# Patch embedding by three products for two neighbouring patches, with its tokens on the partitions, and one set of statistics for two layernorms in a row

## The chip, the core and the metric

The kernel runs on one core of a Trainium2 chip. The metric is the time of one execution on the device in microseconds (us), as the median of three runs. All data are fp32.

The core's engines have queues of their own and run each queue in order. TensorE (PE in the profile, its weight loads PEld) multiplies matrices, VectorE (DVE) and ScalarE (ACT) do elementwise work and reductions, GpSimd (POOL) does small or slow elementwise work, and SyncE (SP) issues transfers. A matmul keeps a stationary operand of 128x128 in the array and streams a moving operand of up to 512 columns through it; its result goes to PSUM. Each fp32 matmul of the program stands in the profile as two instructions, each transpose as one.

## The reference, cut to what matters

```python
# tokenizer: patches of 16 steps, 8 apart, of x [4, 64, 512, 64] (batch, channel, time, variable)
xp = pad(x, 8 more steps at the end, mode="edge")
patches = xp[:, :, idx, :]                        # idx = n * 8 + 0..15, n = 0..63
xf = rfft(patches over the 16 steps, norm="ortho")   # 9 frequencies
h = concat([xf.real, xf.imag]) @ W.T              # [4, 64 variables x 64 patches, 256]

# layer 0: attention with a decaying memory, then an MLP
a = layernorm(h)                                  # first of two in a row, no gain
y = layernorm(a) * g1 + b1
q, k, v = y @ Wq.T + bq, y @ Wk.T + bk, y @ Wv.T + bv
mem[t] = decay * mem[t - 1] + k[t] * v[t]         # over the 4096 tokens of a batch
a = a + q * mem
a = a + relu((layernorm(a) * g2 + b2) @ W1.T + b1) @ W2.T + b2
h = h + a

# experts: the best two of eight, weights by softmax
t = layernorm(h)
h = h + t + sum over e of combine[:, e] * (gelu(t @ w1[e]) @ w2[e])
```

A layernorm subtracts the mean over 256 features and divides by sqrt(variance + 1e-5).

## The kernel before

The DFT is linear, so it is folded into the embedding's weights at the start: `weff[(h c), m, d]`, with `m = 0..7` for the steps of a patch in two halves of four (L90 to L95, 128 VectorE instructions). A token is then the sum over eight `m` of products with 128 rows (two sub-steps times 64 channels) of x.

Each batch has 4096 tokens, cut into 8 blocks of 512 (`BLK`, four tiles of 128, `TT = 4`); there are 32 blocks in all. The tokens run over variables first and patches second. One batch of x lies in SBUF as `xt` (a single buffer, L64); `load_x` for the next batch waits until the last block of this one has read it.

The work of a block is in two generators, whose `yield`s cut it into steps. `attention` (L165) has nine steps: 0 the embedding, features on the partitions (L174, two times eight matmuls with 512 columns, copied with a permutation at L181); 1 eight transposes to tokens (L190, L191) and two layernorms in a row (`z`, `zz`); 2 transposes of `zz` to features (`to_features`, L150); 3 k, v, the scan and q (L162, L212); 4 eight transposes back (L230), the residual, a layernorm, and GpSimd's additions to h (L235, L236); 5 transposes; 6 the MLP's first product (L162 with `w_sb`, activations into the buffer `aT`, L244); 7 its second product (L250), the sum (L257) and a layernorm; 8 transposes of those tokens to `tokT` and the routing (`route`, matmuls L273, 17 small VectorE instructions, `comb`).

`experts` (L305) has nine steps too: the hidden layer of expert 0 (`hidden`, L162 with `ew_sb` and the gelu at L313); then the transposes of `comb` (L321, copied to `combT`, L323), the biases (L328), and for each expert the second product (L337), the weighted sum into h (L346) and the hidden layer of the expert after next. The output goes out in one transfer per block (L354).

What runs beside what is set by the last loop: the experts of a block run step by step between the steps of the next block's attention, experts first in each step. Each engine's queue follows roughly from this order.

```python
for _ in zip_longest(before, attention(state, xt, blk, carry)):
    pass
before = experts(b=b, blk=blk, **state)
```

A layernorm is `bn_stats` and `bn_aggr` for each of four tiles on VectorE (L136, L137), the reciprocal root by `pow` on GpSimd (L139, L140), and four normalisations on VectorE (L142). PSUM has four buffers named `mm`, three named `tm` and one named `sm`. The pool `one` has one buffer for each name.

## Time and profile before

| | |
|---|---|
| median of three runs | 4033.25 us (4033.03 to 4033.52) |
| span of the profiled execution | 4034.0 us |
| mean granted TensorE clock | 0.982 of full speed |
| TensorE busy | 3835.9 us, 95% |
| VectorE busy | 1315.3 us, 33% |
| ScalarE busy | 882.2 us, 22% |
| GpSimd busy | 413.4 us, 10% |
| read from and written to HBM | 43.49 MB, 16.78 MB |

A row of the groups of instructions reads: line, engine, operation, tiles written and read, shapes, count, then busy time in us and mean ns of one, then the engine's idle time ahead of them and what ended it. A row in order of time reads: start in us, duration in us, engine, line, operation, tiles, and in brackets the idle time ahead of it and what ended it. Consecutive equal instructions are merged, and a matmul's duration overlaps with the next one's. A row of the busy time of stretches reads: the stretch, its length, busy us and instructions of PE, PEld, DVE, ACT and POOL, the granted TensorE clock, the DMA share and GB/s.

### The profile page before, as it was taken

What the parts mean: (1) busy time and instruction counts of PE and PEld (TensorE: products, weight loads), DVE (VectorE), ACT (ScalarE), POOL (GpSimd) and SP (SyncE); (2) the same over time, 40 slices, a digit from 0 to 9 for tenths busy, and PEclk for the clock granted to TensorE, in tenths of its full rate; (3) what the DMA queues carried; (4) which work ended last, traced back from release to release, by engine and by line L of the source; (5) the groups of instructions that cost most, each with busy time, mean ns of one, the idle gap of its engine ahead of it and who ended that gap; (6) DMA issues with size and microseconds to landing.
All of it is one profiled execution on the core that took longest, in us unless ns stands there. A gap on an engine that the chain in (4) does not pass through costs nothing. (4 is left out here: it accounts for less than half of the span.)

```text
span 4034.0 us, 32892 instructions
## 1 busy us (share of the span) xinstructions
PE 3835.9 (95%) x13184; PEld 2380.1 (59%) x13184; DVE 1315.3 (33%) x3712; ACT 882.2 (22%) x1248; POOL 413.4 (10%) x559
## 2 busy tenths in 40 slices
PE   2899999999999999999999999999999999999999
PEld 1466566665566565666665665656566656666566
DVE  5223332233333233322333322333233333223232
ACT  0122212222222222122222222222222221222222
POOL 0111110110101110101101011101011010011010
PEclk9899999999999999999999999999999999999999
DMA  6000000004000000001200000000400000000000
GB/s 178 0 6 1 6 6 6 6 6 85 6 6 6 6 1 6 6 6 38 58 1 6 6 6 6 6 1 6 90 6 6 1 6 6 6 6 6 1 6 11
DMA packets 61561, 62.37 MB, mean 15 GB/s; under 512 B 3800, under 2 KB 61152, under 8 KB 61408
## 3 DMA queue, kind: packets, MB, share of 16 engines
q1 hardware_dynamic: 52352, 50.86, 5.3%
q10 hardware_dynamic: 9056, 9.41, 0.9%
q8 instruction: 103, 1.69, 0.2%
q14 instruction: 50, 0.41, 0.0%
HBM read 43.49 MB, written 16.78 MB: 15 GB/s over the span
## 5 line engine op out<-in xcount | busy, mean ns | idle before, releaser
L337 PE MATMUL tm<-ew_sb,ge 128*128 128x256 f32 x4096 | 957.3, 388 | 0.0
L162 PE MATMUL mm<-tokT,ew_sb 128*128 128x512 f32 x2048 | 934.6, 597 | 0.0
L337 PEld LDWEIGHTS tm<-ew_sb,ge 128*128 128x128 f32 x4096 | 789.1, 196 | 145.4 <-issue 43.1
L346 DVE SCALAR_TENSOR_TENSOR h<-tm,comb,h 128x256 f32<-128x256 f32 x1024 | 451.4, 475 | 943.0 <-PE tm L337 942.0
L313 ACT ACTIVATE ge<-mm,vec 128x512 f32<-128x512 f32 x512 | 348.4, 687 | 1334.8 <-PE mm L162 1334.4
L162 PEld LDWEIGHTS mm<-tokT,ew_sb 128*128 128x128 f32 x2048 | 382.8, 191 | 363.8 <-issue 353.1
L174 PE MATMUL mm<-xt,weff 128*128 128x512 f32 x1024 | 447.7, 595 | 63.4 <-DMA xt<-in_x 63.4
L162 PE MATMUL mm<-hT,w_sb 128*128 128x512 f32 x1024 | 447.6, 595 | 0.7 <-ACT hT L154 0.7
L250 PE MATMUL tm<-w_sb,aT 128*128 128x256 f32 x2048 | 447.2, 379 | 0.0
L250 PEld LDWEIGHTS tm<-w_sb,aT 128*128 128x128 f32 x2048 | 389.1, 190 | 53.3 <-issue 0.5
L174 PEld LDWEIGHTS mm<-xt,weff 128*128 128x128 f32 x1024 | 195.7, 191 | 310.0 <-issue 245.0
L162 PEld LDWEIGHTS mm<-hT,w_sb 128*128 128x128 f32 x1024 | 195.6, 191 | 247.3 <-issue 238.2
L162 PE MATMUL mm<-hT,wqkv_sb 128*128 128x512 f32 x768 | 336.6, 594 | 0.2 <-ACT hT L154 0.2
L139 POOL TENSOR_SCALAR rstd<-mv 128x4 f32<-128x4 f32 x128 | 29.2, 228 | 2583.4 <-DVE mv L137 2583.4
L150 PE MATMUL mm<-ident,zz 128*128 128x128 f32 x768 | 178.6, 342 | 119.0 <-DVE zz L142 119.0
L162 PEld LDWEIGHTS mm<-hT,wqkv_sb 128*128 128x128 f32 x768 | 146.5, 191 | 184.8 <-issue 176.3
L150 PEld LDWEIGHTS mm<-ident,zz 128*128 128x128 f32 x768 | 107.8, 163 | 226.2 <-DVE zz L142 166.6
L244 ACT ACTIVATE aT<-mm,vec 128x512 f32<-128x512 f32 x256 | 175.9, 687 | 266.8 <-PE mm L162 266.8
L152 ACT COPY tokT<-mm 128x512 f32<-128x512 f32 x64 | 34.4, 589 | 686.7 <-PE mm L150 686.7
L235 POOL TENSOR_TENSOR h<-h,z 128x256 f32<-128x256 f32 x128 | 90.2, 726 | 914.8 <-ACT ge L313 867.9
L257 DVE TENSOR_TENSOR h<-tm,h 128x512 f32<-128x512 f32 x64 | 44.3, 692 | 379.2 <-PE tm L250 379.2
L181 ACT COPY ret<-mm 128x512 f32<-128x512 f32 x64 | 66.8, 1043 | 401.9 <-PE mm L174 401.9
(61 smaller groups left out, 1858.9 us busy)
## 6 DMA issues: line engine op xcount, KB each, us to landing
xt<-in_x SPq DMA_DIRECT2D x32, 1024.0 KB, 18.5
out<-h SPq DMA_DIRECT2D x32, 512.0 KB, 2.9
ew_sb<-in_ew ACTq DMA_DIRECT2D x2, 2048.0 KB, 31.1
w_sb<-in_w ACTq DMA_DIRECT2D x2, 1024.0 KB, 20.4
wf<-in_wtok ACTq DMA_DIRECT2D x2, 576.0 KB, 12.4
wf<-in_wtok ACTq DMA_DIRECT2D x2, 448.0 KB, 14.2
wqkv_sb<-in_wqkv ACTq DMA_DIRECT2D x1, 768.0 KB, 16.6
xt<-in_x SPq DMA_DIRECT2D x8, 64.0 KB, 14.3
```

The costliest lines, as they stand in the source:

```text
L150: nc.tensor.transpose(ps[:, ts(t, P)], src[:, t, ts(k, P)], ident)
L152: nc.scalar.copy(dst[:, k, :], ps)
L162: nc.tensor.matmul(ps, lhsT=w[:, k, ts(m, P)], rhs=rhs[:, k, :], start=k == 0, stop=k == KD - 1)
L174: nc.tensor.matmul(ps, lhsT=weff[:, m, ts(k, P)], rhs=xt[:, n0 : n0 + N, j * V + v0 : j * V + v0 + nv], start=m == 0, stop=m == 7,)
L181: nc.scalar.copy(hF[:, k, :].rearrange("p (v n) -> p n v", n=N), ps.rearrange("p (n v) -> p n v", n=N))
L235: nc.gpsimd.tensor_tensor(h[:, t, :], h[:, t, :], z[:, t, :], ALU.add)
L244: nc.scalar.activation(aT[:, m, :], ps, AF.Relu, bias=vec[:, MB1 + m : MB1 + m + 1])
L250: nc.tensor.matmul(ps[:, i, :], lhsT=aT[:, k, ts(t2 * 2 + i, P)], rhs=w2_sb[:, k, :], start=k == 0, stop=k == KH - 1,)
L257: nc.vector.tensor_tensor(h[:, ts(t2, 2), :], ps, h[:, ts(t2, 2), :], ALU.add)
L313: nc.scalar.activation(ge[:, m, :], ps, AF.Gelu, bias=vec[:, c : c + 1])
L337: nc.tensor.matmul(ps[:, i, :], lhsT=ge[:, k, ts(t2 * 2 + i, P)], rhs=ew2_sb[:, e, k, :], start=k == 0, stop=k == KD - 1,)
L346: nc.vector.scalar_tensor_tensor(h[:, t, :], ps[:, i, :], comb[:, t, e : e + 1], h[:, t, :], ALU.mult, ALU.add)
```

## The change

Two neighbouring patches, even and odd, share half of their steps: the second half of the even one is the first half of the odd one. With x0, x1, x2 for three consecutive groups of eight steps and W0, W1 for the two halves of the weights, the two tokens are x0 W0 + x1 W1 and x1 W0 + x2 W1. The change computes (x0 - x1) W0, (x2 - x1) W1 and, for both, x1 (W0 + W1).

- `wsum` (W0 + W1) is made once at the start.
- A new first step of `attention` makes the two differences on VectorE and a copy of x1 on ScalarE, for four sub-steps each, into a tile in the buffer named `aT`, in the order of the tokens.
- The embedding's matmuls have these as the stationary operand and the weights as the moving one, so that tokens come out on the partitions. The transposes at L190 and the permuted copies at L181 go. Each sum of two products is added to the common one on VectorE.
- The tiles of tokens are now even and odd patches apart; `hT` is written and `ret` read with a stride of 2, so that the scan has the tokens in order, and the output has two transfers per block.
- The first two layernorms use one set of statistics: the second one's variance is v / (v + eps), so both reciprocal roots come from v.
- `attention` has ten steps now and `experts` still nine.
- The scan writes into `ks`; the tile `mem` goes.

The diff, without the comments that it drops:

```diff
+        wsum = const.tile([P, J, D], F32)
+        nc.vector.tensor_tensor(wsum, weff[:, 0:J, :], weff[:, J:, :], ALU.add)
...
+    def layernorms(once, twice, src):
+        st = small.tile([P, TT, 6], F32, name="st")
+        mv = small.tile([P, TT, 2], F32, name="mv")
+        for t in range(TT):
+            nc.vector.bn_stats(st[:, t, :], src[:, t, :])
+            nc.vector.bn_aggr(mv[:, t, :], st[:, t, :])
+        rstd2 = small.tile([P, 2, TT], F32, name="rstd2")
+        nc.gpsimd.tensor_scalar(rstd2[:, 0, :], mv[:, :, 1], EPS, None, ALU.add)
+        nc.gpsimd.tensor_scalar(rstd2[:, 1, :], mv[:, :, 1], 1.0 + EPS, EPS * EPS, ALU.mult, ALU.add)
+        nc.gpsimd.tensor_tensor(rstd2, rstd2, mhalf2, ALU.pow)
+        for i, dst in ((1, twice), (0, once)):
+            for t in range(TT):
+                nc.vector.tensor_scalar(
+                    dst[:, t, :], src[:, t, :], mv[:, t, 0:1], rstd2[:, i, t : t + 1], ALU.subtract, ALU.mult
+                )
...
     def attention(state, xt, blk, carry):
         v0, nv = blk * BLK // N, BLK // N
-        hF = one.tile([P, KD, BLK], F32, name="ret")
-        for k in range(KD):
-            ps = p_mm.tile([P, BLK], F32, name="mm")
-            for m in range(8):
-                n0, j = m // J, m % J
-                nc.tensor.matmul(ps, lhsT=weff[:, m, ts(k, P)],
-                    rhs=xt[:, n0 : n0 + N, j * V + v0 : j * V + v0 + nv], start=m == 0, stop=m == 7)
-            nc.scalar.copy(
-                hF[:, k, :].rearrange("p (v n) -> p n v", n=N), ps.rearrange("p (n v) -> p n v", n=N)
-            )
+        xs = one.tile([P, 3, J, BLK // 2], F32, name="aT")
+        for j in range(J):
+            seg = xt[:, :, j * V + v0 : j * V + v0 + nv]
+            even, odd, after = seg[:, 0:N:2, :], seg[:, 1:N:2, :], seg[:, 2 : N + 1 : 2, :]
+            dst = [xs[:, i, j, :].rearrange("p (v n) -> p n v", n=N // 2) for i in range(3)]
+            nc.vector.tensor_tensor(dst[0], even, odd, ALU.subtract)     # L202
+            nc.vector.tensor_tensor(dst[1], after, odd, ALU.subtract)    # L203
+            nc.scalar.copy(dst[2], odd)                                  # L204
         yield
         h = two.tile([P, TT, D], F32, name="h")
-        for t2 in range(TT // 2):
+        ps = p_tm.tile([P, 2, D], F32, name="tm")
+        for u in range(TT // 2):
+            for j in range(J):
+                nc.tensor.matmul(
+                    ps[:, u, :], lhsT=xs[:, 2, j, ts(u, P)], rhs=wsum[:, j, :], start=j == 0, stop=j == J - 1
+                )
+        ms = one.tile([P, 2, D], F32, name="ms")
+        nc.scalar.copy(ms, ps)
+        for u in range(TT // 2):
             ps = p_tm.tile([P, 2, D], F32, name="tm")
             for i in range(2):
-                for k in range(KD):
-                    nc.tensor.transpose(ps[:, i, ts(k, P)], hF[:, k, ts(t2 * 2 + i, P)], ident)
-            nc.scalar.copy(h[:, ts(t2, 2), :], ps)
+                for j in range(J):
+                    nc.tensor.matmul(ps[:, i, :], lhsT=xs[:, i, j, ts(u, P)],
+                        rhs=weff[:, i * J + j, :], start=j == 0, stop=j == J - 1)
+            nc.vector.tensor_tensor(
+                h[:, ts(u, 2), :], ps, ms[:, u : u + 1, :].to_broadcast([P, 2, D]), ALU.add
+            )
+        yield
         z = one.tile([P, TT, D], F32, name="z")
-        layernorm(z, h)
         zz = two.tile([P, TT, D], F32, name="zz")
-        layernorm(zz, z)
+        layernorms(z, zz, h)
         yield
         hT = one.tile([P, KD, BLK], F32, name="hT")
-        to_features(hT, zz, G1, B1)
+        to_features(hT, zz, G1, B1, scan=True)     # written with a stride of 2
...
-                    nc.tensor.transpose(ps[:, i, ts(k, P)], ret[:, k, ts(t2 * 2 + i, P)], ident)
+                    nc.tensor.transpose(ps[:, i, ts(k, P)], ret[:, k, t2 * 2 * P + i : (t2 + 1) * 2 * P : 2], ident)
...
-        nc.sync.dma_start(out=out[b, ts(blk, BLK), :].rearrange("(t p) d -> p t d", p=P), in_=h)
+        to = out[b, ts(blk, BLK), :].rearrange("(u q r) d -> u q r d", q=P, r=2)
+        for u in range(TT // 2):
+            nc.sync.dma_start(out=to[u], in_=h[:, ts(u, 2), :])
```

In the changed kernel the transposes of `to_features` stand at L172, the feature products at L188, the routing matmuls at L309, the transposes of `comb` at L357, the biases at L364, the experts' second product at L373 and the MLP's second product at L286.

## The prediction

> **What bounds the kernel now.** I read the page's totals first, then TensorE's instructions in order of time in a block in the middle and in the first block, then the granted clock.

> ```profile
> PE 3835.9 (95%) x13184; PEld 2380.1 (59%) x13184; DVE 1315.3 (33%) x3712; ACT 882.2 (22%) x1248; POOL 413.4 (10%) x559
> ...
> L174 PE MATMUL mm<-xt,weff 128*128 128x512 f32 x1024 | 447.7, 595 | 63.4 <-DMA xt<-in_x 63.4
> ...
> L152 ACT COPY tokT<-mm 128x512 f32<-128x512 f32 x64 | 34.4, 589 | 686.7 <-PE mm L150 686.7
> ...
> L181 ACT COPY ret<-mm 128x512 f32<-128x512 f32 x64 | 66.8, 1043 | 401.9 <-PE mm L174 401.9
> ```

> TensorE bounds it; VectorE and ScalarE are idle most of the time. The embedding (L174) is 32 instructions a block. The two copies show what a permuted write costs on ScalarE: 1043 ns against 589 for as many elements.

> ```profile
> 1916.68 3.60 PE L162 MATMUL mm<-tokT,ew_sb 128*128 128x512 f32 x8
> 1922.28 2.19 PE L150 MATMUL mm<-ident,zz 128*128 128x128 f32 x8 [2.00 <-DVE zz L142]
> 1924.26 4.52 PE L337 MATMUL tm<-ew_sb,ge 128*128 128x256 f32 x16
> 1928.62 3.60 PE L162 MATMUL mm<-tokT,ew_sb 128*128 128x512 f32 x8
> ...
> 1983.68 13.98 PE L250 MATMUL tm<-w_sb,aT 128*128 128x256 f32 x64
> 1997.49 3.62 PE L337 MATMUL tm<-ew_sb,ge 128*128 128x256 f32 x16
> 2001.33 1.74 PE L150 MATMUL mm<-ident,zz 128*128 128x128 f32 x8 [0.22 <-DVE zz L142]
> ...
> 2005.97 2.82 PE L162 MATMUL mm<-tokT,ew_sb 128*128 128x512 f32 x6
> 2008.63 13.90 PE L174 MATMUL mm<-xt,weff 128*128 128x512 f32 x32
> 2022.36 0.60 PE L321 MATMUL sm<-ident,comb 128*8 128x128 f32 x4
> ```

> Costs are best read from start to start. The embedding takes 2022.36 - 2008.63 = 13.73 us. The block has two places to watch. At 1922 the transposes wait for two layernorms in a row. At 1997 an expert's product (L337) covers the layernorm between L250 and the next transposes, so only 0.39 us stay open. From 2008.63 to the same row 15 blocks later is 1843.2 us: a block is 122.88 us.

> The first block has no expert beside it and shows that place uncovered (the third row is VectorE's, the others TensorE's):

> ```profile
> 134.78 13.98 PE L250 MATMUL tm<-w_sb,aT 128*128 128x256 f32 x64
> 152.43 1.97 PE L150 MATMUL mm<-ident,zz 128*128 128x128 f32 x8 [3.67 <-DVE zz L142]
> ...
> 148.79 0.69 DVE L257 TENSOR_TENSOR h<-tm,h 128x512 f32<-128x512 f32 x1 [5.21 <-PE tm L250]
> ...
> 160.00 5.20 PE L162 MATMUL mm<-tokT,ew_sb 128*128 128x512 f32 x6
> 165.03 13.90 PE L174 MATMUL mm<-xt,weff 128*128 128x512 f32 x32
> ```

> The busy time of stretches gives the clock there (third number from the end):

> ```profile
> 151.20:165.00 13.80, 12.11 (x32) 7.81 (x33) 4.59 (x21) 3.27 (x5) 3.06 (x2) 0.51 0.00 1
> 2001.40:2004.80 3.40, 3.16 (x16) 1.89 (x16) 2.02 (x6) 2.12 (x3) 2.36 (x1) 1.00 0.11 38
> 2045.80:2049.20 3.40, 3.40 (x13) 3.00 (x13) 0.67 (x2) 1.45 (x2) 0.00 (x0) 0.54 0.00 0
> ```

> After the uncovered wait of 3.67 us the clock was halved for 13.8 us, four steps of about 3.41. The wait of 2.00 us in each later block halves it for one step. 122.88 is 36 such steps: the block has settled on the grid of the clock.

> **The change, part by part, for one block, at full clock.**

> Embedding: three products of 256 tokens in four steps are 24 matmuls, 48 instructions of 128x256. L250 gives 13.81 / 64 = 0.216 us each, so 10.36 against 13.73: -3.37. The eight transposes at L190 go (0.87 us from start to start): -0.87.

> One set of statistics, and a step more: the block has ten steps against the experts' nine, and the order of instructions shows two experts' products and two hidden layers, 2 x (3.46 + 3.43) = 13.8 us, between the embedding and the transposes of zz. The chain behind it (sum, statistics, three POOL instructions, four normalisations, four expert updates) is about 7 us, so the wait goes. Before, 1920.11 (end of L162) to 1924.26 was 4.15 us for transposes that need 0.87: -3.28. The slowed L337 behind it (4.36 instead of 3.46) is whole again: -0.90. The next layernorm's wait (0.96 us) is untouched; what is late there is POOL's adds to h.

> The price of the extra step: the last expert's product now runs before the MLP's second product, and the transposes of tok (L172) follow that directly. Block 0 shows this wait: 148.76 to 152.43, 3.67 us. Into its VectorE chain the new order puts two of the next block's eight subtractions (L202, L203) ahead of the last statistic, because they write the buffer named aT and may start only once the MLP has read it. No row shows a strided subtraction of 128x256. Half of L257 (0.69 for 128x512) is 0.35; times 1043/589, what a permuted write cost ScalarE, it is 0.62. I take 0.6, since the writes step 128 bytes. The wait is then 3.67 + 1.2 = 4.9 instead of 0.39: +4.5. A third subtraction stands between the statistics and the normalisations, beside POOL's rstd (1.47 us from last statistic to first normalisation), and is hidden; if it is not, its 0.6 makes the wait 5.5 (upper end).

> [...]

> Routing: its VectorE chain (17 small instructions, 3.85 us) had the embedding as cover. Now 12 instructions of L188 (5.2 us) cover it and one matmul covers the copy of combT (0.68): +0.1; without that cover 4 us.

> At no cost: the other five subtractions run while TensorE transposes and routes; ScalarE's four copies (0.3 to 0.6 each) end before tokT's, which wait 4.9 us anyway; ms (0.59) lies under 6.9 us of products; the stride of 2 in hT lies under 6.9 us of expert work; in ret it could slow eight weight loads (0.14 us each) by about 1 us at most. VectorE gains 6 us and loses 2 in 123. SP issues two outputs for one; x is released earlier than before and has over 100 us to land (18.5 each).

> Full clock: 122.88 - 3.37 - 0.87 - 3.28 - 0.90 + 4.5 + 0.1 = 119.1 us.

> **The clock.** An idle stretch of 4.9 us is longer than a step of the clock, and behind it come transposes and 128x8 matmuls, which in block 0 didn't bring the clock back. Block 0 gives the price. From transposes to the last routing matmul 152.43 to 160.00 is 7.57, at full clock (2001.33 to 2005.97) 4.64: 2.9. The three matmuls behind took 5.03 instead of 2.66: 2.4. Sum 5.3. The first part is paid wherever the clock falls before the transposes; the second is half of one to two steps, 1.7 to 3.4. In some alignments the clock falls only later, so I take 5.0, with 2.9 and 6.3 as ends. A block is 124.1.

> **Ends.** At the start TensorE waits for x until 63.38 and the first zz transposes come at 90.79. Now wsum and the subtractions follow the DFT weights (done at 67.4), while half of the products can go ahead; I put the end of the embedding near 81 and the transposes, one layernorm earlier (4.7 us) and without the L190 transposes, at 85: -5.8, give or take 3. Block 0 then ends L250 at 143.0 instead of 148.76. Behind the last L250 (3963.57) were 70.4 us; now 70.4 - 3.84 + 4.9 + 5.0 = 76.5.

> Sum: 143.0 + 31 x 124.1 + 76.5 = **4067 us**. The page gives 4034.0 us as the span of the profiled execution and nothing outside it; the median of the three runs, 4033.25, is 0.02% less, which I leave out.

> **Rivals.** *Cheap clock.* The drop costs no more than the one step per block of before: 0.90 for L337 and 0.50 for the transposes. Then a block is 120.5 and the time 143.0 + 31 x 120.5 + 72.9 = 3951, faster. It decides where the price is under 3.5 us, that is where the window with the routing matmuls counts as work. For it: in 2001.40:2004.80 such a stretch kept a clock of 1.00. Against it: in block 0 the same instructions did not bring it back. Chance 0.21.
> *Settled on the grid.* The price adjusts so that the block stays at 36 steps, as it did before: 122.88, a price of 3.8: 143.0 + 3809.3 + 75.3 = 4028, no change that can be told (0.2%, 8 us, is about the least). Chance 0.19.
> *Long tail.* The subtractions cost more than 0.9 or the third joins, and the block settles at 37 steps, 126.3: 143.0 + 3915 + 79 = 4137. Chance 0.10.
> The forecast keeps 0.5.

> **Range and chances.** Price 2.9: a block is 122.0 and the time 3999. Wait 4.9 with 6.3: 4108; wait 5.5 with 5.3: 4095. So 3999 to 4110, which takes in the grid and leaves out most of the cheap and the long case. Of the forecast's half nearly all is slower by over 0.2%; it gives a little to both sides: faster 0.23, same 0.15, slower 0.62.

> **What would show it.** Right: transposes of tok waiting 4.4 to 5.5 us behind L286 in every block; no wait at the zz transposes; 48 embedding instructions in about 10.4 us; a halved clock behind L286 for two to four steps. Wrong: a block under 122 us or a clock back within one step (cheap); subtractions over 0.9 us (long); a new wait at L357 or L364 over 1 us (routing cover too short); embedding waiting for aT or ms.

## The result, and the profile after

The changed kernel took 4057.26 us (median of four runs, 4056.77 to 4058.88) against 4033.39 for the kernel before on the same chip: a ratio of 1.0059, interval 1.0044 to 1.0073. It is slower by 0.6%. The forecast was 4067.

The profiled execution spans 4057.0 us. Two rows of its page, the totals and the transposes of L172 (all three sorts of them in a block, 768 instructions), and last the row of the same transposes in the kernel before:

```profile
PE 3780.9 (93%) x13440; PEld 2513.5 (62%) x13440; DVE 1494.8 (37%) x3777; ACT 867.8 (21%) x1280; POOL 409.0 (10%) x528
...
L172 PE MATMUL mm<-ident,zz 128*128 128x128 f32 x768 | 147.0, 327 | 184.1 <-DVE zz L147 179.6
...
L150 PE MATMUL mm<-ident,zz 128*128 128x128 f32 x768 | 178.6, 342 | 119.0 <-DVE zz L142 119.0
```

TensorE is busy for 55.0 us less than before (3835.9), even at a lower mean clock (0.950 instead of 0.982). It stands idle for 276.1 us (4057.0 - 3780.9) instead of 198.1. So the change took work away and gave more back in waits: 179.6 us of the idle time end with a normalisation (L147) that feeds L172, where it was 119.0.

TensorE's instructions in order of time, in a block in the middle, show where:

```profile
1909.08 3.62 PE L210 MATMUL tm<-wsum,aT 128*128 128x256 f32 x16
...
1919.44 3.62 PE L373 MATMUL tm<-ew_sb,ge 128*128 128x256 f32 x16
...
1933.21 1.04 PE L172 MATMUL mm<-ident,zz 128*128 128x128 f32 x8
1934.09 3.62 PE L373 MATMUL tm<-ew_sb,ge 128*128 128x256 f32 x16
...
1989.25 13.98 PE L286 MATMUL tm<-w_sb,aT 128*128 128x256 f32 x64
2007.66 1.75 PE L172 MATMUL mm<-ident,zz 128*128 128x128 f32 x8 [4.43 <-DVE zz L147]
...
2015.02 7.16 PE L188 MATMUL mm<-tokT,ew_sb 128*128 128x512 f32 x12
2022.02 0.60 PE L357 MATMUL sm<-ident,comb 128*8 128x128 f32 x4
```

The embedding takes 1919.44 - 1909.08 = 10.36 us. The transposes of zz at 1933.21 have no bracket: they wait for nothing, and the next product starts 0.88 us later. L286 occupies TensorE until 1989.25 + 13.81 = 2003.06, and the transposes of tok come at 2007.66: 4.60 us open, where the kernel before had 0.39. From those transposes to the end of the routing at 2015.02 it is 7.36 us, against 4.64 at full clock before, and the twelve instructions of L188 behind it take 2022.02 - 2015.02 = 7.00.

The busy time of stretches, cut where the clock changes in this block (columns: stretch, length, then busy us and instructions of PE, PEld, DVE, ACT and POOL, granted clock, DMA share, GB/s):

```profile
2001.54:2004.95 3.41, 1.69 (x8) 1.14 (x6) 1.68 (x5) 1.64 (x4) 0.00 (x0) 1.00 0.00 0
2004.95:2008.36 3.41, 0.70 (x5) 0.46 (x5) 2.28 (x9) 0.32 (x1) 1.37 (x2) 1.00 0.00 0
2008.36:2011.77 3.41, 2.95 (x9) 1.88 (x9) 3.41 (x4) 2.36 (x3) 2.51 (x1) 0.50 0.00 0
2011.77:2015.19 3.42, 3.42 (x16) 3.01 (x15) 1.20 (x3) 0.00 (x0) 0.00 (x0) 0.50 0.00 0
2015.19:2018.60 3.41, 3.41 (x5) 1.34 (x6) 2.84 (x15) 2.20 (x3) 0.00 (x0) 0.50 0.00 0
```

The clock falls during the transposes, at 2008.36, and is halved for three steps of 3.41; at 2018.60 it is whole again. Each block has one such halved stretch behind L286, of three or four steps (10.24 or 13.65 us, 16 blocks each). Before the change, each block but the first had one at the transposes of zz, one step long.

VectorE's instructions between L286 and the normalisations show what filled the wait:

```profile
2003.27 0.69 DVE L293 TENSOR_TENSOR h<-tm,h 128x512 f32<-128x512 f32 x1 [5.21 <-PE tm L286]
2003.87 0.59 DVE L202 TENSOR_TENSOR aT<-xt 128x256 f32<-128x256 f32 x1
2004.30 0.73 DVE L141 BATCH_NORM_STATS2 st<-h 128x6 f32<-128x256 f32 x2
...
2005.03 0.56 DVE L203 TENSOR_TENSOR aT<-xt 128x256 f32<-128x256 f32 x1
2005.43 0.16 DVE L142 BATCH_NORM_AGGREGATE mv<-st 128x2 f32<-128x6 f32 x1
2005.51 0.56 DVE L202 TENSOR_TENSOR aT<-xt 128x256 f32<-128x256 f32 x1
2007.19 1.38 DVE L147 TENSOR_SCALAR zz<-h,mv,rstd 128x256 f32<-128x256 f32 x4 [1.13 <-POOL rstd L145]
...
2008.93 2.71 DVE L202 TENSOR_TENSOR aT<-xt 128x256 f32<-128x256 f32 x1
```

Two of the next block's subtractions (L202, L203) stand ahead of the last statistic (L142), and a third, at 2005.51, between it and the normalisations (L147). From the start of one to the next instruction is 2004.30 - 2003.87 = 0.43 and 2005.43 - 2005.03 = 0.40 us.

### The profile page after: what moved, and what is told of

It reads as the page before. It is cut to its first block, busy times and chain, and to the rows that moved or that the text cites. A ratio compares the mean times of both kernels' runs of the same rounds, so it can differ in the third digit from the quotient of the medians.

```text
span 4057.0 us, 33585 instructions
## 1 busy us (share of the span) xinstructions
PE 3780.9 (93%) x13440; PEld 2513.5 (62%) x13440; DVE 1494.8 (37%) x3777; ACT 867.8 (21%) x1280; POOL 409.0 (10%) x528
## 4 chain that ended last, share of the span: by engine, by line
PE 87%; POOL 6%; DVE 4%; issue 1%; ACT 0%; DMA 0%; ACTq 0%; DVEq 0%; POOLq 0%
PE mm L188 40%; PE tm L373 19%; PE tm L286 11%; PE tm L219 5%; PE mm L172 3%; PE tm L210 3%; PE sm L309 3%; POOL h L271 2%; POOL h L272 2%; POOL rstd L145 2%; PE tm L364 2%; DVE weff L93 1%; DVE zz L147 1%; DVE z L267 1%; DVE h L293 0%
## 5 line engine op out<-in xcount | busy, mean ns | idle before, releaser
L188 PE MATMUL mm<-tokT,ew_sb 128*128 128x512 f32 x2048 | 1029.5, 646 | 0.0
L373 PE MATMUL tm<-ew_sb,ge 128*128 128x256 f32 x4096 | 929.2, 380 | 0.0
L373 PEld LDWEIGHTS tm<-ew_sb,ge 128*128 128x128 f32 x4096 | 768.7, 190 | 152.2 <-issue 50.6
L188 PEld LDWEIGHTS mm<-tokT,ew_sb 128*128 128x128 f32 x2048 | 416.5, 208 | 404.8 <-issue 394.2
L286 PE MATMUL tm<-w_sb,aT 128*128 128x256 f32 x2048 | 447.2, 379 | 0.0
L188 PE MATMUL mm<-hT,w_sb 128*128 128x512 f32 x1024 | 446.4, 594 | 0.7 <-ACT hT L180 0.7
L286 PEld LDWEIGHTS tm<-w_sb,aT 128*128 128x128 f32 x2048 | 389.1, 190 | 53.3 <-issue 0.5
L188 PEld LDWEIGHTS mm<-hT,w_sb 128*128 128x128 f32 x1024 | 195.1, 191 | 233.3 <-issue 230.1
L188 PE MATMUL mm<-hT,wqkv_sb 128*128 128x512 f32 x768 | 337.7, 596 | 0.7 <-ACT hT L180 0.7
L172 PE MATMUL mm<-ident,zz 128*128 128x128 f32 x768 | 147.0, 327 | 184.1 <-DVE zz L147 179.6
L172 PEld LDWEIGHTS mm<-ident,zz 128*128 128x128 f32 x768 | 104.6, 161 | 258.1 <-DVE zz L147 174.0
L188 PEld LDWEIGHTS mm<-hT,wqkv_sb 128*128 128x128 f32 x768 | 146.9, 191 | 186.0 <-issue 176.9
L219 PE MATMUL tm<-weff,aT 128*128 128x256 f32 x1024 | 226.2, 379 | 0.0
L219 PEld LDWEIGHTS tm<-weff,aT 128*128 128x128 f32 x1024 | 194.6, 190 | 26.5
L210 PE MATMUL tm<-wsum,aT 128*128 128x256 f32 x512 | 118.6, 386 | 70.7 <-DVE wsum L98 70.7
L293 DVE TENSOR_TENSOR h<-tm,h 128x512 f32<-128x512 f32 x64 | 44.2, 691 | 378.1 <-PE tm L286 378.1
L226 DVE TENSOR_TENSOR h<-tm,ms 128x512 f32<-128x512 f32 x64 | 44.2, 691 | 356.1 <-issue 285.6
L204 ACT COPY aT<-xt 128x256 f32<-128x256 f32 x128 | 62.9, 637 | 512.6 <-PE tm L286 512.2
```

What stands on the lines that cost most here:

```text
L172: nc.tensor.transpose(ps[:, ts(t, P)], src[:, t, ts(k, P)], ident)
L188: nc.tensor.matmul(ps, lhsT=w[:, k, ts(m, P)], rhs=rhs[:, k, :], start=k == 0, stop=k == KD - 1)
L210: nc.tensor.matmul(ps[:, u, :], lhsT=xs[:, 2, j, ts(u, P)], rhs=wsum[:, j, :], start=j == 0, stop=j == J - 1)
L219: nc.tensor.matmul(ps[:, i, :], lhsT=xs[:, i, j, ts(u, P)], rhs=weff[:, i * J + j, :], start=j == 0, stop=j == J - 1,)
L286: nc.tensor.matmul(ps[:, i, :], lhsT=aT[:, k, ts(t2 * 2 + i, P)], rhs=w2_sb[:, k, :], start=k == 0, stop=k == KH - 1,)
L373: nc.tensor.matmul(ps[:, i, :], lhsT=ge[:, k, ts(t2 * 2 + i, P)], rhs=ew2_sb[:, e, k, :], start=k == 0, stop=k == KD - 1,)
```

## The experiments

The theory is that the kernel loses because the extra step uncovers the layernorm behind L286, and that the halved clock behind that wait costs as much again. Its rivals: that the subtractions in the buffer `aT` are the loss (a matter of buffers and not of steps); that the clock would be halved anyway and costs little; and that the gain at the transposes of zz came from the merged statistics and not from the extra step. Each result is the median, with its ratio to the kernel before on the same chip. The line numbers of TensorE's instructions shift by one to three between these kernels (the filling takes L296, and in the run on the kernel before the transposes are L169).

**Work in place of the wait.** Ten matmuls whose result nobody uses stand behind the MLP's second product; the rest is the changed kernel.

```diff
+        fill = p_tm.tile([P, 2, D], F32, name="tm")
+        for i in range(10):
+            nc.tensor.matmul(fill[:, i % 2, :], lhsT=ident, rhs=w2_sb[:, 0, :], start=True, stop=True)
```

> The changed kernel with ten matmuls of 128x256 added behind the MLP's second product (identity times w2, result not read), 20 instructions or 4.3 us of TensorE work where it waits 4.6 us. The output doesn't use them. Theory (the wait and the halved clock are two prices): the wait is still paid, as work, but the clock stays at 1.00 behind it, a block is about 118.8 us and the time 3895 to 3915, about 150 us less for more work. Rival (no separate price of the clock; the wait and its neighbours are all there is): 4055 to 4065.

Measured: 3905.74 us, 0.9682 [0.9668, 0.9696]. TensorE at the same place:

```profile
2049.37 4.48 PE L296 MATMUL tm<-w_sb,ident 128*128 128x256 f32 x20
2054.06 1.73 PE L172 MATMUL mm<-ident,zz 128*128 128x128 f32 x8 [0.21 <-DVE zz L147]
...
2057.22 1.62 PE L312 MATMUL sm<-rw_sb,tokT 128*128 128x8 f32 x14
2058.70 5.40 PE L188 MATMUL mm<-tokT,ew_sb 128*128 128x512 f32 x12
```

The filling (L296) starts where L286 ends. The transposes come no earlier (2054.06 - 2049.37 = 4.69 us, against 4.60), yet the kernel is 151.5 us faster with more work. The fourteen routing matmuls take 1.62 us, where the changed kernel had 2.99, and the twelve of L188 5.40 instead of 7.16. The mean clock is 0.996. That is the price of the clock by itself: a block takes 118.95 us here and 123.74 in the changed kernel; the longer open place counts the other way, so the price is 123.74 - 118.95 + 0.09 = 4.88 us a block. The cheap clock is refuted, and so is a clock that would be halved anyway.

**The differences in buffers that come free earlier.** They go into the buffers `kv`, `ks` and `ret`, which nobody reads at that time, and not into `aT`. Ten steps are kept.

```diff
-        xs = one.tile([P, 3, J, BLK // 2], F32, name="aT")
+        xs = [one.tile([P, J, BLK // 2], F32, name=name) for name in ("kv", "ks", "ret")]
...
```

> The changed kernel, ten steps, with the differences and the copy in the buffers kv, ks and ret instead of aT: these are free long before the MLP's second product, so the subtractions leave the chain behind it. Theory (two subtractions of 0.44 us and a little waiting of GpSimd beside the third are 0.93 of the 4.6 us): the wait at tok's transposes falls to 3.67 us; with the halved clock as it is now a block would be 122.8, and 122.88 is 36 steps of the clock, where it can settle: 4020 to 4035. Rival (the subtractions cost nothing where they stood; the wait is all the layernorm): 4050 to 4060.

Measured: 4030.85 us, 0.9991 [0.9981, 1.0]. The transposes of tok:

```profile
2097.43 13.98 PE L286 MATMUL tm<-w_sb,aT 128*128 128x256 f32 x64
2115.08 1.41 PE L172 MATMUL mm<-ident,zz 128*128 128x128 f32 x8 [3.67 <-DVE zz L147]
```

The open place is 2115.08 - 2097.43 - 13.81 = 3.84 us, 0.76 less than in the changed kernel, and equal to block 0's before the change, counted in the same way (152.43 - 134.78 - 13.81). The last block of the changed kernel, which has no next block's subtractions in its way, has the same 3.84. So the subtractions cost 0.76 us a block, a sixth of the open place, and the time is 26 us less than the changed kernel's. What stays is the bare layernorm, and the clock still falls behind it: it is 0.61 in the 7.42 us from 2115.08 and 0.70 in the 7.50 us from 2122.50, which makes 10.3 us at half speed, three steps. Its mean of 0.957 makes 346 us at half speed in the whole run (2 x 0.043 x 4028.7), enough for as much in each of the 32 blocks. The blocks stand exactly 122.88 us apart, the 36 steps of before: the same row 14 blocks later starts at 3835.40. This is what the prediction's rival on the grid described, reached with a wait shorter by 0.76 us.

**Nine steps again.** The embedding and the two layernorms share a step, so that the last expert's product again stands behind L286.

```diff
             nc.vector.tensor_tensor(
                 h[:, ts(u, 2), :], ps, ms[:, u : u + 1, :].to_broadcast([P, 2, D]), ALU.add
             )
-        yield
         z = one.tile([P, TT, D], F32, name="z")
```

> The step between the embedding and the layernorms goes: attention has nine steps again and the last expert's product stands behind the MLP's second product. Theory (the tenth step costs the cover of the tok layernorm, 4.6 us of waiting and some 4.9 us of halved clock per block): the wait there falls from 4.4 to about 1.2 us, the clock is halved for at most one step of 3.4 us per block, a block is 115.5 to 117 us and the time 3800 to 3850. Rival (the loss comes from the new work, the strided subtractions or the products with other operands, wherever the last expert stands): a block stays near 123.7 and the time near 4057.

Measured: 3830.06 us, 0.9497 [0.9472, 0.9522]. The transposes of tok in a block in the middle; the expert's product behind L286 starts at 2024.45:

```profile
2029.00 1.52 PE L172 MATMUL mm<-ident,zz 128*128 128x128 f32 x8 [0.93 <-DVE zz L147]
```

One `yield` turns a loss of 0.6% into a gain of 5%. The product covers 3.46 us of the 2029.00 - 2024.45 = 4.55 behind L286, and 1.09 stay open. The clock still falls behind it in this block: the fourteen routing matmuls take 3.00 us and the fourteen L188 behind them 9.26, where the blocks before and after, behind waits of 0.89 and 0.91, have 1.62 and 6.25. From the transposes to those of comb it is 15.76 us here and 10.74 in the block after. The 5.02 between them are 10.04 us at half speed, about three steps, where at most one had been expected. The mean clock of the profiled execution is 0.983. The runs spread over 25 us.

**Nine steps, joined at another place.** The differences and the products share a step instead.

```diff
             nc.scalar.copy(dst[2], odd)
-        yield
         h = two.tile([P, TT, D], F32, name="h")
```

> The other way to nine steps: the step between the differences and the embedding's products goes. Theory: as without the other step, the last expert covers the tok layernorm, 3800 to 3850; the embedding now also covers the routing, but its products may wait for the differences, which may start only when the MLP's second product is done (up to 2 us a block more). Rival (new work to blame): near 4057.

Measured: 3778.65 us, 0.9367 [0.9353, 0.9381], 21 us below the range expected. TensorE at the same place (L308 is the routing):

```profile
1988.32 1.52 PE L172 MATMUL mm<-ident,zz 128*128 128x128 f32 x8 [0.92 <-DVE zz L147]
1989.68 1.03 PE L209 MATMUL tm<-wsum,aT 128*128 128x256 f32 x4
1990.54 0.28 PE L308 MATMUL sm<-rw_sb,tokT 128*128 128x8 f32 x2
```

The wait is the same as in the kernel above, 0.92 against 0.93. What differs is that the common product of the next block is in the queue by then: four of its instructions (L209) run while ScalarE copies tokT, and the routing behind them, at 1990.54, does not wait. The mean clock is 0.997, which leaves about 23 us at half speed in the whole run (2 x 0.003 x 3777.3). Behind the MLP's second product the fourteen routing matmuls take 1.62 us in this block, in the two after it, in block 0 and in the last one, so the clock is whole there. Why it holds here behind the same wait is not shown by a run.

**The merged statistics alone**, in the kernel before: its embedding, its nine steps. The helper `layernorms` and its constant come with it.

```diff
-        layernorm(z, h)
         zz = two.tile([P, TT, D], F32, name="zz")
-        layernorm(zz, z)
+        layernorms(z, zz, h)
...
```

> The kernel before with the one set of statistics for two layernorms alone, nine steps, old embedding. Theory: the wait of 2.0 us at the zz transposes and the halved step behind it go, 4.2 us a block: 118.7 us, time about 3900 to 3910. Rival (the layernorms are off the path and the clock's step falls elsewhere in the block): 4025 to 4035.

Measured: 3915.12 us, 0.9706 [0.969, 0.9722], 5 us above the range. The transposes of zz, in their place between two experts' products, wait for nothing:

```profile
1982.76 1.04 PE L169 MATMUL mm<-ident,zz 128*128 128x128 f32 x8
```

**The merged statistics undone**, in the changed kernel: two separate layernorms, ten steps.

```diff
-        layernorms(z, zz, h)
+        layernorm(z, h)
+        layernorm(zz, z)
```

> The changed kernel with the two layernorms computed separately again, ten steps kept. Theory (13.8 us of expert work between the embedding and the zz transposes cover two layernorms as well as one; the longer chain is about 10 us): no wait appears, 4050 to 4065, so that in this order the one set of statistics brings nothing. Rival (the merged statistics carry their 4.2 us a block here too): about 4185.

Measured: 4047.93 us, 1.0035 [1.0022, 1.0048]. The transposes of zz:

```profile
2053.26 1.04 PE L172 MATMUL mm<-ident,zz 128*128 128x128 f32 x8
```

No bracket: even two layernorms in a row are covered here. So with ten steps the merged statistics save nothing that is on the path, while in nine steps they alone gave 2.9%. The time is 2 us below the range and some 9 us less than with them; the intervals of the two ratios overlap a little (1.0044 to 1.0048). The granted clock shows where the profiled executions differ: its mean is 0.953 here and 0.950 there, which makes 380 and 406 us at half speed (2 x 0.047 x 4045.2 and 2 x 0.050 x 4057.0). Half of the difference is 13 us, and the spans differ by 11.8. Why the clock is halved for less time here stays open.

**Both mended.** Differences and products in one step, and the buffers that come free earlier.

```diff
-        xs = one.tile([P, 3, J, BLK // 2], F32, name="aT")
+        xs = [one.tile([P, J, BLK // 2], F32, name=name) for name in ("kv", "ks", "ret")]
...
             nc.scalar.copy(dst[2], odd)
-        yield
...
```

> Both repairs: differences and products in one first step (nine steps) and the buffers kv, ks and ret. Theory: behind the last expert's product the wait falls from 0.92 to about 0.25 us, and the products no longer wait for the differences; a block falls by 0.7 to 1.2 us to about 113.5 and the time to 3740 to 3760, with hardly any halved clock. Rival (the waits of the differences are covered there already, or the subtractions disturb the scan where they now stand): 3770 to 3790.

Measured: 3765.36 us, 0.9335 [0.9321, 0.9349]: between the two ranges, and the best of all. The transposes of tok:

```profile
2095.55 1.73 PE L172 MATMUL mm<-ident,zz 128*128 128x128 f32 x8 [0.22 <-DVE zz L147]
```

The wait of 0.92 has become the 0.22 that the kernel before had. That is 0.69 us in 32 blocks, 22 us, of which 13 are seen in the time. The rest is given back behind the wait: from the transposes to the end of the embedding it is 17.22 us here (2095.55 to 2112.77) and 16.94 with the buffer `aT` (1988.32 to 2005.26).

## Why the prediction was right

The time came out 10 us below the forecast, with its mechanism. Its sum (4066.6) and the measured one differ in three terms: the start +3.75, 31 blocks by 123.74 - 124.1 = -0.36 each, -11.2, and the end -2.3. That makes 4056.9 against a span of 4057.0.

- *Embedding, -3.37 us:* 10.36 us for the 48 instructions, as worked out. The row of L250, for other tensors but the same shape, gave the price exactly.
- *Transposes at L190 and the wait at zz, -0.87, -3.28 and -0.90:* gone, as said. The prediction gave the cover to two experts' products and the merged statistics together; the run with two statistics shows that the products alone suffice.
- *The tail, an open place of 4.9 us:* 4.60. The mechanism was right to the instruction: L286's uncovered chain, plus two subtractions ahead of the last statistic. The mis-sized term is the two subtractions. They were put at 0.6 each, by what a permuted write cost ScalarE. That is what the profile gives as the duration of one (0.59 and 0.56), but the next instruction starts after 0.43 and 0.40. From the start of L293 to the end of the last statistic it is 2.32 us here and 1.70 in the run with free buffers, so the two cost 0.62 and not 1.2; with the third it is the 0.76 of that run. Half of L257's 0.69, the other end, was nearer. What the stride of 128 bytes costs VectorE isn't shown: no run makes these differences without it.
- *The third subtraction, hidden:* nearly. From the last statistic's end to the first normalisation it is 2007.19 - 2005.59 = 1.60 us, against 1.47 where no subtraction stood there. So it cost 0.13.
- *Routing cover, +0.1:* the biases (L364, at 2023.41) start 0.95 us behind the two L188 that hide the copy of combT; two of them take 2 x 5.23 / 12 = 0.87 at full clock, so 0.08 stay.
- *Block at full clock, 119.1:* with work in place of the wait a block took 118.95, of which 0.09 is the longer open place; so 118.86, which is 119.1 with the wait corrected.
- *Price of the clock, 5.0:* 4.88. The step that carried it was reading block 0, the one block of the kernel before in which the place was uncovered. The first part (transposes and routing) was put at 2.9 and is 7.36 - 4.64 = 2.7 in the block above; the twelve L188 behind it take 7.00, against 5.23 where the wait was filled, and 1.8 is within the 1.7 to 3.4 of the second part. That block has a stretch of three steps; over all blocks but the first and the last the two places average 7.49 and 7.37, which makes 2.9 and 2.1. The sum read from block 0 was 5.3; it was lowered to 5.0 for alignments whose share was not worked out, so that it came within 0.12 is in part luck.
- *The start, 143.0:* 146.75, a miss of 3.75 of the 5.8 promised. Here half of the products were to go ahead of `wsum`:

```profile
70.65 6.53 PE L210 MATMUL tm<-wsum,aT 128*128 128x256 f32 x16 [70.65 <-DVE wsum L98]
77.02 7.07 PE L219 MATMUL tm<-weff,aT 128*128 128x256 f32 x32
88.65 1.97 PE L172 MATMUL mm<-ident,zz 128*128 128x128 f32 x8 [4.56 <-DVE zz L164]
```

The step that failed is this overlap. TensorE's queue has the common product first, and that is the one which needs `wsum`; nor could the others have gone ahead, because VectorE has `wsum` ahead of the subtractions in its queue and starts the first of these at 70.47. So the products begin at 70.65, and they end at 84.1 instead of 81. Of these 3.1 us, 1.9 have another cause: the input of the DFT weights came later (VectorE waits for it until 19.6, before until 17.7), and the weights were done at 69.3 instead of 67.4. Inputs come late without the new embedding too: in the run on the kernel before with the merged statistics the first matmul, which waits for x, starts at 67.40, and in the kernel before at 63.38. The layernorm behind the products adds 4.56 instead of 4. GpSimd's root is longer than it was, 1666 ns for the eight columns of L161, where the four of L145 take 1.04 us.

- *At no cost, the stride of 2 in `ret`:* the eight transposes take 0.95 us from start to start (1958.16 to 1959.11) against 0.87 (1949.24 to 1950.11), so 0.08 a block.
- *The grid:* the prediction had the block either free (124.1) or at 36 steps (122.88). It is a mixture. In the trace's granted clock the halved stretches of the blocks begin 122.88 us apart three times and 126.29, one step more, the fourth time: (3 x 122.88 + 126.29) / 4 = 123.73.

The upper end of the predicted wait, 5.5 us, had the third subtraction's 0.6 in the chain, beside GpSimd's root. It cost 0.13: GpSimd's first instruction (L144) starts 0.20 us after it, inside it, and takes 0.33 us, against 0.23 in the run with free buffers. Some three us later a subtraction beside GpSimd took far longer. GpSimd's addition to h in the same block, in order of time:

```profile
2008.65 2.51 POOL L296 TENSOR_TENSOR h<-h,zz 128x1024 f32<-128x1024 f32 x1 [1.50 <-DVE zz L147]
```

It starts at 2008.65 and ends at 2011.16. The subtraction that VectorE starts at 2008.93, inside it, takes 2.71 us instead of 0.6 and ends 0.48 behind it. TensorE transposes and routes at that time, so it costs nothing. The prediction did not see this one.

## What to carry to other kernels

An edit that adds a step to one of two interleaved programs shifts which work covers which wait: before crediting its savings, find every place where the other program's work stood, and price the place that is left bare by a block that already shows it bare (the first, without a neighbour). Price with it what the clock does behind an idle stretch; here that was 4.88 us for 4.60 us of idling, and ten useless matmuls bought it back. The same arithmetic in nine steps, with buffers that come free early, is 6.6% faster than the kernel before, so the loss was one of order and not of the change itself.

## What the runs showed of the hardware

Where the clock falls in every block, the blocks can settle at a whole number of steps: 36 of them (122.88 us) in the kernel before, and in the changed kernel with free buffers too, though their work differs. There a block has 10.3 us at half speed instead of 3.41, and what the change saved is gone. The changed kernel itself mixes 36 and 37 steps. What decides between settling and mixing is not shown.
